# Last layer of a four-layer convolution and attention kernel: bias rows in the third group, six fillings before the third convolution, two convolutions in the third gathering step

## The chip, the core and the metric

The kernel runs as one program on one core of a Trainium2 chip. The metric is the device time of one execution in microseconds (us). The times shown are of three runs and of one profiled execution.

The engines are named as in the profile: PE is TensorE (PEld its weight loads), DVE is VectorE, ACT is ScalarE, POOL is GpSimd, SP is SyncE, which here only issues transfers.

## The reference

The input is one image of 512 channels and 64 x 64 pixels in float32. Four layers follow each other, each as `x = x + layer(group_norm(x))`: an attention by distances with 8 heads, two layers of gated depthwise 7 x 7 convolutions, and a linear attention. The change is in the last one:

```
qkv0 = affine(conv1x1(x, w_qkv))                 # 768 channels
agg  = affine(depthwise5x5(qkv0)) * w_pw*s_pw + b_pw
q, k, v = split(concat(qkv0, agg), 3)            # 512 channels each
q, k = relu(q) + eps, relu(k) + eps
z    = einsum(mean(k), q) + eps
vk   = einsum('bcn,bdn->bcd', v/sqrt(N), k/sqrt(N))
y    = einsum(vk, q) / z * g_norm + bt_norm + v
out  = affine(conv1x1(y, w_proj))
```

## The kernel before, in words

The image X (4 chunks of 128 channels, 4096 pixels) stays in SBUF. The last layer, `_linear_attention` (L1597), goes in these stages; a matmul in float32 stands in the trace as two records.

**Groups.** The 1 x 1 convolution to 768 channels is done for pairs of output chunks i = 0, 2, 4 and pairs of pixel blocks k = 0 to 3. One such pair of pairs is a "group (i,k)" of seven steps (`_Seven.steps`, in the order p1, p5, p2, p7, p6, p3, p4), each with two chunks of matmuls. Their operands are sums of weights (`w_sum`, made in `summed`) and differences of pixel blocks (`diff`, made in `differences`). The banks are `ps_vk` vk0 to vk3, one to each of the four sums of a group, and the next group takes them again. The results are kept (`keep`, L1789, ACT, in the pool tmp of 7 buffers), combined (L518, L522) and put (L1162 on ACT; L1169 and L1172 on DVE) into planes, which are stored to DRAM tensors G (L1151) by ACT or POOL.

**The list of steps.** From group (0,1) on the 77 steps lie in one list, `made`, in the order (0,1), (0,2), (0,3), (2,3), (2,2), (2,1), (2,0), (4,0) to (4,3). A group can bring a list of other pieces, one to a step (`also`); a piece is run just ahead of its step. `fill(n)` runs the next n steps of the list.

**Convolutions.** The depthwise 5 x 5 convolution of chunk i, half image hf, is `conv(i, hf)`: twelve of them, each in two parts of 128 matmul records. Each part takes two loads (`_PlaneConv.load`): taps T, a gathered S from G (L1198, issued by SP), and two shifted copies of S inside SBUF, one on ACT (L1205) and one on DVE (L1203). After a part its two banks (`ps_mm`, 4 in all) are transposed to the tile `turned` (L1259), and after the second part in four pieces on to the tiles `agg` (L1268); ACT then scales these (L1874). `convs(units, between)` runs convolutions, and after each part the next piece of `between`. The agg, w_sum, diff, k and q tiles come from one pool, kv, of 33 buffers.

The order is: 29 fillings; convolutions (0,0) and (1,0) with five fillings after each of their four parts; four fillings; convolutions (2,0) and (3,0) with six after each part; then (0,1), (4,0), (5,0) with 16 "early" products of v and w_proj between their parts, 1, 3, 3, 3, 3, 3. Then come the gathering steps q = 0 to 3 of the first half, each of four steps (`step`): a transposition of k and v blocks (L1930), the products vk of the step before, and a product with w_proj. Steps q = 0, 1, 2 hold one convolution each, (1,1), (2,1), (3,1), and q = 3 holds (4,1) and (5,1). The steps of the second half follow with no convolution, and then the output.

**Bias of the projection.** `pbias` is the sum over w_proj rows times bt_norm, scaled and shifted. `bias_row` and `row` load 128 x 512 rows through POOL's queue into the tmp pool; `bias(o)` multiplies (L1696) and reduces (L1697) one, `added` (L1699) finishes. `scaled_out` (L1680) multiplies w_proj by the row `s_row`, loaded by ACT's queue into a buffer of its own. The rows are loaded with group (2,2) and the biases made with (2,1), between the parts of the first two convolutions.

**Order of instructions.** Matmuls and a few others are pinned to the order in which the program names them (`keep_in_program_order`). All other instructions are put in order on their engines by the framework, which also places the tiles in the pools' buffers and adds the waits.

Of the kernel before, what the change touches and what calls it, by code (L numbers as in the profile page):

```python
# [10 lines left out]
FP = mybir.dt.float32  # L11
# [5 lines left out]
P = 128  # L17
# [1077 lines left out]
class _PlaneConv:  # L1095
# [117 lines left out]
    def conv(self, i, hf, wT, finish, dst, primed=False):  # L1213

        nc, f = self.nc, self.f
        if not primed:
            self.ahead(i, hf, wT)
        for r0 in range(0, f.nr, f.rounds):  # L1220
            ps = [self.psum.tile([P, BLK], FP, tag="mm", name="ps_cv") for _ in range(2)]
            for r in range(r0, r0 + f.rounds):
                if r % f.run == 0 and r > r0:
                    yield
                if r % self.nl == 0:
                    if r + f.rounds < f.nr:
                        self.ready.append(self.load(i, hf, wT, r + f.rounds))
                    w, S = self.ready.pop(0)
                for b in range(f.by * f.bx):
                    by, bx = divmod(b, f.bx)  # L1230
                    for rho in range(2):
                        rows = ts(rho, 64)
                        for g in range(4):
                            self.matmul(
                                ps[rho][ts(g, 32), ts(r - r0, f.n)].rearrange(
                                    "p (r w) -> p r w", w=f.w
                                ),
                                w[rows, r % self.nl, g, b, :],
                                S[rows, r % self.nl, g, :].rearrange(
                                    "p (r w) -> p r w", w=f.fw  # L1240
                                )[:, by : by + f.part, bx : bx + f.w],
                                start=(b == 0),
                                stop=(b == f.by * f.bx - 1),
                            )
            for rho in range(2):
                c0 = (rho * f.nr + r0) * f.ch
                if f.parts == 1:
                    out = dst.rearrange("p (l b c) -> p c b l", l=f.planes, c=32)[
                        :, c0 : c0 + f.rounds
                    ]  # L1250
                    src = ps[rho].rearrange("p (r b l) -> p r b l", r=f.rounds, l=f.planes)
                else:
                    out = self.turned[:, :, :, c0 : c0 + f.rounds * f.ch].rearrange(
                        "p b l (r c) -> p r b l c", c=f.ch
                    )
                    src = ps[rho].rearrange(
                        "p (r b l c) -> p r b l c", r=f.rounds, l=f.planes, c=f.ch
                    )
                nc.vector.transpose(out, src)  # L1259
            if r0 + f.rounds < f.nr:  # L1260
                yield
        for q in range(4):
            if f.parts == 1:
                d = dst[:, ts(q, N // 4)]
                nc.vector.transpose(d, d)  # L1265
            else:
                d = dst[q]
                nc.vector.transpose(  # L1268
                    d.rearrange("p (h x r w) -> p x r w h", h=2, x=f.phx, r=f.part),
                    self.turned[:, :, ts(q, f.phx), :].rearrange("p b l c -> p l b c"),  # L1270
                )
            finish(d)
            if f.parts == 1 or q == 3:
                yield
# [322 lines left out]
def _linear_attention(ctx, tc, a, X, vcol, vall, ident, gmask, small, centered, stats, norm, F, Z, out):  # L1597
# [45 lines left out]

    with ExitStack() as st:

        kvp = st.enter_context(tc.tile_pool(name="kv", bufs=33))
        ps_vk = st.enter_context(tc.tile_pool(name="ps_vk", bufs=1, space=PSUM))
        ps_mm = st.enter_context(tc.tile_pool(name="ps_mm", bufs=4, space=PSUM))
        pc = _PlaneConv(st, tc, f, F, ps_mm, NL, 4, True, nc.gpsimd, 2)
# [14 lines left out]
        def weights(i):  # L1664
# [6 lines left out]
        pbias = small.tile([P, NC], FP, tag="pbias", name="pbias")  # L1671
        step_p = small.tile([P, NC // 2], FP, tag="step_p", name="step_p")

        s_row = lq.tile([P, C], FP, tag="s_row", name="s_row")
        nc.scalar.dma_start(
            out=s_row, in_=bass.AP(a["L3_sp"].tensor, a["L3_sp"].offset, [[0, P], [1, C]])
        )

        def scaled_out(c):
            nc.vector.tensor_mul(w_proj[:, c], w_proj[:, c], s_row)  # L1680

        w_bt = []

# [75 lines left out]
        def summed(i):  # L1759
            ss = [kvp.tile([P, BLK], FP, tag="kv", name="w_sum") for _ in range(2)]  # L1760
            ss = [
                t.rearrange("p (n c m) -> p n c m", n=2, c=2)[:, n] for t in ss for n in range(2)
            ]
            wsum[i] = ss
            for _ in seven.sums(nc.vector, w_qkv[i], w_qkv[i + 1], ss):
                pass

        def differences(k, eng):

            def begin():  # L1770
                t = [
                    [flat(kvp.tile([P, BLK], FP, tag="kv", name="diff")) for _ in range(2)]
                    for _ in range(4)
                ]
                diff[k] = t, seven.differences(eng, view(k), t)

            def piece(n):
                if n == 0:
                    begin()
                for _ in range(2):  # L1780
                    next(diff[k][1])

            return [lambda n=n: piece(n) for n in range(4)]
# [11 lines left out]
        def group(i, k, also=()):  # L1795

            steps = []

            def begin():
                steps.extend(  # L1800
                    seven.steps(
                        w_qkv[i], w_qkv[i + 1], wsum[i], diff[k][0], view(k), bank,
                        lambda j, ps: keep(i, j, ps),
                        lambda m, n, ps, more: put(i + m, 2 * k + n, ps, more),
                    )
                )

            def step(n):
                if n == 0:
                    begin()  # L1810
                if n < len(also):
                    also[n]()
                steps[n]()

            return [lambda n=n: step(n) for n in range(7)]

        def centers(k):
            return [lambda: taken(2 * k), lambda: taken(2 * k + 1)]
# [24 lines left out]
            [lambda: taken(2), lambda: taken(3), lambda: summed(0)] + differences(1, dve),  # L1843
        )
        centered.began()
        made = group(0, 1, centers(2) + differences(2, dve))
        made += group(0, 2, centers(3) + differences(3, dve))
        made += group(0, 3, [lambda: summed(2)])
        scales = [lambda c=c: scaled_out(c) for c in range(NC)]
        rows = [bias_row] + [lambda o=o: row(a["L3_w_projT"][:, o]) for o in range(2)]  # L1850
        biases = [lambda n=n: n % 2 or bias(n // 2) for n in range(2 * NC - 1)]
        made += group(2, 3, [more_weights] + scales)
        made += group(2, 2, differences(0, dve) + rows)
        made += group(2, 1, biases)
        made += group(2, 0, [lambda: summed(4)] + differences(2, pool) + [added])
        made += group(4, 0)
        made += group(4, 1, differences(3, pool))
        made += group(4, 2)
# [7 lines left out]
            return [lambda n=n: fill(n) for n in ns]  # L1866

        def conv(i, hf, primed):
            agg[i, hf] = [kvp.tile([P, BLK], FP, tag="kv", name=f"agg{i}") for _ in range(4)]

            def affine(t):
                late.append(
                    lambda: tc.keep_in_program_order(
                        nc.scalar.activation(  # L1874
                            t, t, AF.Relu if i < 2 else AF.Identity,
                            bias=beta[:, i : i + 1], scale=alpha[:, i : i + 1],
                        )
                    )
                )

            return pc.conv(i, hf, a["L3_T"], affine, agg[i, hf], primed)

        late = []

# [99 lines left out]
            early = [lambda o=o: part(o, 0, 2) for o in range(NC)]  # L1984
            return prepare, turned, [lambda t=t: step(t) for t in range(QT)], early

        def both(*pieces):
            return lambda: [f() for f in pieces]

        def project_two(q0):  # L1990

            def v(c, n):
# [75 lines left out]

        fill(29)
        convs([(0, 0), (1, 0)], fills(5, 5, 5, 5))  # L2070
        fill(4)
        blks = {(hf, q): gather(hf, q) for hf in range(2) for q in range(4)}

        def prepare(hf, q):
# [5 lines left out]
        def steps(hf, q):  # L2080
            return list(blks[hf, q][2])

        convs([(2, 0), (3, 0)], fills(6, 6, 6, 6))

        early = [f for q in range(4) for f in blks[0, q][3]]
        convs(
            [(0, 1), (4, 0), (5, 0)],
            [
                early[0],
                both(*early[1:4]),  # L2090
                both(*early[4:7], prepare(0, 0)),
                both(*early[7:10]),
                both(*early[10:13]),
                both(*early[13:]),
            ],
        )
        vkp = [ps_vk.tile([P, C], FP, tag=f"vk{c}", name=f"vkp{c}") for c in range(NC)]
        for q in range(3):
            s = steps(0, q)
            convs([(q + 1, 1)], [s[0], both(prepare(0, q + 1), s[1])] + s[2:], 1)  # L2100
        s = steps(0, 3)
        convs(
            [(4, 1), (5, 1)],
            [s[0], s[1], both(prepare(1, 0), s[2]), turned(1, 0, 0, 1), s[3]],
            1,
        )

        km = wp.tile([P, NC], FP, tag="km", name="km")
        kmb = wp.tile([P, NC, 32], FP, tag="kmb", name="kmb")
# [327 lines left out]
```

## Time and profile before

| | us |
|---|---|
| three runs | 3759.53, 3754.57, 3759.23 |
| median | 3759.23 |
| profiled execution | 3754.97 |
| its span | 3753.1 |
| TensorE busy | 3689.7 (98%) |
| VectorE busy | 2751.0 (73%) |
| ScalarE busy | 2058.1 (55%) |
| POOL busy | 181.7 (5%) |

The mean granted TensorE clock is 0.996. The last layer by stages, in us of the span:

| stage | from | to | PE busy | DVE busy | granted clock | GB/s |
|---|---|---|---|---|---|---|
| groups (0,1) to (2,3) | 3176.2 | 3224.3 | 48.10 | 33.78 | 1.00 | 139 |
| convolutions (0,0), (1,0) | 3224.3 | 3270.3 | 40.06 | 30.79 | 0.93 | 166 |
| four fillings, convolutions (2,0), (3,0) | 3270.3 | 3340.7 | 68.09 | 45.51 | 0.98 | 176 |
| (0,1), (4,0), (5,0) | 3340.7 | 3382.8 | 39.82 | 29.81 | 1.00 | 188 |
| gathering, first half | 3382.8 | 3509.5 | 121.79 | 82.83 | 0.99 | 104 |
| gathering, second half | 3509.5 | 3628.0 | 118.50 | 57.59 | 1.00 | 44 |
| output | 3628.0 | 3753.1 | 119.14 | 98.52 | 1.00 | 111 |

How to read it: a line of the timeline gives the start, the length, the engine, the line of the code, the operation, the output and its inputs, the number of records, and in brackets the idle time ahead of it with what ended it. A busy time below the length of a stage is idle time of that engine. The granted clock is a share of TensorE's full clock.

### The profile page before, as it was taken

The page shows a single profiled execution, that of the slowest core. Times are in us where ns is not written, and L with a number is a line of the kernel's source. Part 1 is how long each engine was busy: PE and PEld are TensorE (multiplying, and loading weights), DVE is VectorE, ACT ScalarE, POOL GpSimd, SP SyncE. Part 2 cuts the span into 40 slices and gives each one's busy share as a digit, 9 for nine tenths or more (in the row PEclk, how much of TensorE's full clock was granted, in tenths as well). Part 3 has the DMA queues.
Part 4 walks back from the last instruction along what each step waited for, and adds up shares of the span by engine and source line. Part 5 has one row for each costly group of instructions (what it writes and reads, how often), then busy time and mean ns, then how long its engine had stood idle before and what let it go on. Part 6 is the DMA issues. An engine that isn't in the chain of part 4 may idle for free. (4 is left out here: it accounts for less than half of the span.)

```text
span 3753.1 us, 81702 instructions
## 1 busy us (share of the span) xinstructions
PE 3689.7 (98%) x35096; PEld 1713.3 (46%) x35096; DVE 2751.0 (73%) x3593; ACT 2058.1 (55%) x2994; POOL 181.7 (5%) x174
## 2 busy tenths in 40 slices
PE   7999999999999999999999999999999999999999
PEld 6544444444464444444333344554445544455543
DVE  6677777777766777777778767776777678666648
ACT  3577774777735777747557546662356632354210
POOL 1000000000000000010000000000000000232222
PEclk9999999999999999999999999999999999999999
DMA  2000000000000000000000026762057620564322
GB/s 102 10 7 7 4 7 12 7 4 7 7 4 10 7 7 4 7 12 7 4 4 7 4 73 196 199 191 60 22 180 196 190 87 31 157 184 111 88 65 93
DMA packets 183470, 222.73 MB, mean 59 GB/s; under 512 B 15800, under 2 KB 124600, under 8 KB 182976
## 3 DMA queue, kind: packets, MB, share of 16 engines
q1 hardware_dynamic: 158752, 158.36, 15.3%
q10 hardware_dynamic: 21312, 48.03, 3.5%
q0 software_dynamic: 3040, 11.08, 0.8%
q8 instruction: 277, 4.54, 0.5%
q14 instruction: 89, 0.73, 0.1%
HBM read 157.51 MB, written 59.90 MB: 58 GB/s over the span
## 5 line engine op out<-in xcount | busy, mean ns | idle before, releaser
L844 ACT ACTIVATE pt<-ps_s,A 128x512 f32<-128x512 f32 x2048 | 1286.2, 687 | 446.9 <-PE ps_s L836 436.8
L836 PE MATMUL ps_s<-O,K 64*64 64x512 f32 x8192 | 1419.3, 589 | 0.0
L1017 DVE TENSOR_TENSOR acc<-acc,pt 128x1024 f32<-128x1024 f32 x960 | 1178.0, 1227 | 324.8 <-ACT pt L844 299.0
L856 PE MATMUL av<-pt,O 64*64 64x512 f32 x4096 | 747.2, 589 | 0.0
L856 PE MATMUL av<-pt,V 64*64 64x512 f32 x4096 | 673.6, 589 | 0.0
L836 PEld LDWEIGHTS ps_s<-O,K 64*64 64x64 f32 x8192 | 438.4, 133 | 514.3 <-issue 464.2
L1205 ACT COPY S<-S 32x1295 f32<-32x1295 f32 (+1 forms) x272 | 341.8, 1256 | 223.0 <-DMA S<-F 107.8
L856 PEld LDWEIGHTS av<-pt,O 64*64 64x64 f32 x4096 | 238.4, 133 | 250.0 <-issue 237.2
L856 PEld LDWEIGHTS av<-pt,V 64*64 64x64 f32 x4096 | 209.3, 133 | 268.4 <-issue 254.0
L1128 PE MATMUL ps<-diff,w_sum 128*128 128x512 f32 x516 | 245.5, 608 | 8.8 <-DVE plane L1172 5.5
L1128 PEld LDWEIGHTS ps_cv<-S,T 64*32 64x32 f32 x13824 | 195.1, 106 | 113.4 <-issue 70.4
L1128 PE MATMUL ps_cv<-S,T 64*32 64x128 f32 x13824 | 234.2, 274 | 7.5 <-issue 2.5
L1128 PE MATMUL ps<-h,w_out_L 128*128 128x512 f32 x512 | 229.6, 600 | 1.5 <-DVE X L1488 1.4
L472 DVE TENSOR_TENSOR diff<-X 128x512 f32<-128x512 f32 x200 | 133.3, 682 | 69.0 <-PE ps L1128 36.8
L400 ACT ACTIVATE X<-X,gn_less 128x512 f32<-128x512 f32 x118 | 75.2, 709 | 153.7 <-DVE gn_less L130 152.8
L1128 PE MATMUL ps<-X,w_in_L 128*128 128x512 f32 x304 | 145.9, 611 | 8.6 <-ACT kept L1410 5.7
L1128 PEld LDWEIGHTS ps<-diff,w_sum 128*128 128x128 f32 x516 | 95.4, 191 | 123.9 <-issue 110.5
L1128 PEld LDWEIGHTS ps<-h,w_out_L 128*128 128x128 f32 x512 | 94.0, 190 | 118.3 <-issue 96.5
L1259 DVE STREAM_TRANSPOSE h<-ps_cv 128x512 f32<-128x512 f32 x112 | 109.3, 1049 | 49.8 <-PE ps_cv L1128 49.3
L1128 PE MATMUL ps<-h,pw_L 128*128 128x512 f32 x320 | 143.7, 599 | 1.7 <-DVE h L1476 1.4
L472 DVE TENSOR_TENSOR diff<-X,diff 128x512 f32<-128x512 f32 x200 | 134.7, 683 | 10.5 <-PE ps L1128 10.4
L1128 PE MATMUL vkp<-kT,vT 128*128 128x512 f32 x256 | 115.2, 592 | 0.0
(284 smaller groups left out, 3361.5 us busy)
## 6 DMA issues: line engine op xcount, KB each, us to landing
T<-in_L_T_dram SPq DMA_DIRECT2D x112, 384.0 KB, 4.2
F<-plane ACTq DMA_DIRECT2D x112, 324.0 KB, 3.5
S<-F SPq DMA_DIRECT2D x224, 162.0 KB, 4.6
S<-G SPq DMA_DIRECT2D x96, 153.0 KB, 4.6
row<-G SPq DMA_DIRECT2D x48, 272.0 KB, 3.3
T<-in_L_T_dram SPq DMA_DIRECT2D x48, 256.0 KB, 4.0
G<-plane POOLq DMA_DIRECT2D x33, 289.0 KB, 2.7
rd<-R SPq DMA_DIRECT2D x64, 128.0 KB, 2.9
```

What stands on the lines that cost most here:

```text
L400: return self.nc.scalar.activation(xs, xs, AF.Identity, bias=less)
L472: yield eng.tensor_tensor(t[j][c], a(c), b(c), ALU.subtract)
L836: nc.tensor.matmul(ps[ts(half, D), ts(h, BLK)], K[rows, t * P + half * D : t * P + (half + 1) * D], QO[pair][rows, cols], start=True, stop ...
L844: exp = nc.scalar.activation(pt[:, ts(h, BLK)], ps[:, ts(h, BLK)], AF.Exp, bias=A[:, t, h : h + 1])
L856: nc.tensor.matmul(av[half][rows, :], v[keys, t * P + h * D : t * P + (h + 1) * D], pt[keys, ts(h, BLK)], start=(t == 0), stop=(t == NT - 1),)
L1017: add = nc.vector.tensor_add(acc, acc if u > 1 else first, pt)
L1128: self.tc.keep_in_program_order(self.nc.tensor.matmul(*args, **kw))
L1205: nc.scalar.copy(second, first)
L1259: nc.vector.transpose(out, src)
```

## The change

- The three row loads are attached to the last step of group (0,2); the four biases and their finish go to steps 2, 3, 5 and 6 of group (0,3). Empty pieces stand between them.
- The row `s_row` has no buffer of its own any more; ACT's queue loads it into a tmp buffer with the first step of group (2,3), and w_proj is multiplied by it with that group's steps 2 to 5.
- Six fillings in place of four stand between the second convolution (1,0) and the third (2,0); after the parts of (2,0) and (3,0) stand 6, 6, 5, 5 in place of four times 6.
- The early products are 1, 2, 3, 3, 3, 4.
- The third gathering step holds convolutions (3,1) and (4,1), the fourth only (5,1).
- An agg tile is taken from its pool only when its piece is transposed, not all four when the convolution begins; the pool kv has 34 buffers.

```diff
-                d = dst[q]
+                d = dst(q)
...
-        kvp = st.enter_context(tc.tile_pool(name="kv", bufs=33))
+        kvp = st.enter_context(tc.tile_pool(name="kv", bufs=34))
...
-        s_row = lq.tile([P, C], FP, tag="s_row", name="s_row")
-        nc.scalar.dma_start(
-            out=s_row, in_=bass.AP(a["L3_sp"].tensor, a["L3_sp"].offset, [[0, P], [1, C]])
-        )
+        def scale_row():
+            t = tmp.tile([P, C], FP, tag="tmp", name="s_row")
+            nc.scalar.dma_start(
+                out=t, in_=bass.AP(a["L3_sp"].tensor, a["L3_sp"].offset, [[0, P], [1, C]])
+            )
+            w_bt.append(t)
...
-            nc.vector.tensor_mul(w_proj[:, c], w_proj[:, c], s_row)
+            nc.vector.tensor_mul(w_proj[:, c], w_proj[:, c], w_bt[-1])
...
-        made += group(0, 2, centers(3) + differences(3, dve))
-        made += group(0, 3, [lambda: summed(2)])
...
-        biases = [lambda n=n: n % 2 or bias(n // 2) for n in range(2 * NC - 1)]
-        made += group(2, 3, [more_weights] + scales)
-        made += group(2, 2, differences(0, dve) + rows)
-        made += group(2, 1, biases)
-        made += group(2, 0, [lambda: summed(4)] + differences(2, pool) + [added])
+        made += group(0, 2, centers(3) + differences(3, dve) + [both(*rows)])
+        biases = [lambda o=o: bias(o) for o in range(NC)]
+        wait = [lambda: None]
+        made += group(
+            0, 3, [lambda: summed(2)] + wait + biases[:2] + wait + [biases[2], both(biases[3], added)]
+        )
+        made += group(2, 3, [both(more_weights, scale_row)] + wait + scales)
+        made += group(2, 2, differences(0, dve))
+        made += group(2, 1)
+        made += group(2, 0, [lambda: summed(4)] + differences(2, pool))
...
-            agg[i, hf] = [kvp.tile([P, BLK], FP, tag="kv", name=f"agg{i}") for _ in range(4)]
+            agg[i, hf] = []
+
+            def rows(q):
+                agg[i, hf].append(kvp.tile([P, BLK], FP, tag="kv", name=f"agg{i}"))
+                return agg[i, hf][q]
...
-        fill(4)
+        fill(6)
...
-        convs([(2, 0), (3, 0)], fills(6, 6, 6, 6))
+        convs([(2, 0), (3, 0)], fills(6, 6, 5, 5))
...
-                both(*early[1:4]),
-                both(*early[4:7], prepare(0, 0)),
-                both(*early[7:10]),
-                both(*early[10:13]),
-                both(*early[13:]),
+                both(*early[1:3]),
+                both(*early[3:6], prepare(0, 0)),
+                both(*early[6:9]),
+                both(*early[9:12]),
+                both(*early[12:]),
...
-        for q in range(3):
+        for q in range(2):
             s = steps(0, q)
             convs([(q + 1, 1)], [s[0], both(prepare(0, q + 1), s[1])] + s[2:], 1)
+        s = steps(0, 2)
+        convs([(3, 1), (4, 1)], [s[0], s[1], both(prepare(0, 3), s[2]), s[3]], 1)
         s = steps(0, 3)
-        convs(
-            [(4, 1), (5, 1)],
-            [s[0], s[1], both(prepare(1, 0), s[2]), turned(1, 0, 0, 1), s[3]],
-            1,
-        )
+        convs([(5, 1)], [s[0], s[1], both(prepare(1, 0), s[2]), turned(1, 0, 0, 1), s[3]], 1)
```

More of the change, by code (lines that the diff above doesn't have):

```diff
@@ L1845, in _linear_attention, with both @@
         centered.began()
-        made = group(0, 1, centers(2) + differences(2, dve))
-        made += group(0, 2, centers(3) + differences(3, dve))
-        made += group(0, 3, [lambda: summed(2)])
+        def both(*pieces):
+            return lambda: [f() for f in pieces]
         scales = [lambda c=c: scaled_out(c) for c in range(NC)]
         rows = [bias_row] + [lambda o=o: row(a["L3_w_projT"][:, o]) for o in range(2)]
-        biases = [lambda n=n: n % 2 or bias(n // 2) for n in range(2 * NC - 1)]
-        made += group(2, 3, [more_weights] + scales)
-        made += group(2, 2, differences(0, dve) + rows)
-        made += group(2, 1, biases)
-        made += group(2, 0, [lambda: summed(4)] + differences(2, pool) + [added])
+        made = group(0, 1, centers(2) + differences(2, dve))
+        made += group(0, 2, centers(3) + differences(3, dve) + [both(*rows)])
[8 more added lines that the diff above has]
+        made += group(2, 0, [lambda: summed(4)] + differences(2, pool))
         made += group(4, 0)
@@ L1879, in affine @@
                 )
-            return pc.conv(i, hf, a["L3_T"], affine, agg[i, hf], primed)
+            return pc.conv(i, hf, a["L3_T"], affine, rows, primed)
         late = []
@@ L1985, in gather @@
             return prepare, turned, [lambda t=t: step(t) for t in range(QT)], early
-        def both(*pieces):
-            return lambda: [f() for f in pieces]
         def project_two(q0):
```

## The prediction, made before the changed kernel ran

> **What bounds the kernel now.** I read the page first: TensorE is busy for 98% of the span, so only its idle time and its slow stretches can be won. The change touches only the last layer (from 3161 us to the end), so next I asked whom TensorE waits for from 3060 us on:
>
> ```profile
> PE ps L1128 <- DVE plane L1172: 5.5, 1, 5.5
> PE ps_t L1930 <- ACT agg L1874: 2.7, 2, 1.5
> PE ps_cv L1128 <- DVE S L1203: 2.2, 2, 1.4
> PE ps_cv L1128 <- DVE turned L1259: 2.0, 2, 1.8
> ```
>
> (us in total, times, longest.) A handful of single waits, none of them a regular pattern. The timeline of TensorE places them; the brackets hold the idle time before a piece:
>
> ```profile
> 3243.05 1.98 PE L1128 MATMUL ps<-diff,w_sum 128*128 128x512 f32 x4 [0.43 <-DVE plane L1169]
> 3252.25 3.75 PE L1128 MATMUL ps<-diff,w_sum 128*128 128x512 f32 x4 [5.50 <-DVE plane L1172]
> ...
> 3284.93 0.42 PE L1128 MATMUL ps_cv<-S,T 64*32 64x128 f32 x8 [0.56 <-ACT S L1205]
> 3286.79 3.53 PE L1128 MATMUL ps_cv<-S,T 64*32 64x128 f32 x120 [1.43 <-DVE S L1203]
> ...
> 3385.17 0.33 PE L1930 MATMUL ps_t<-ident,agg 128*128 128x128 f32 x1 [1.46 <-ACT agg L1874]
> ...
> 3494.59 3.41 PE L1128 MATMUL ps_cv<-S,T 64*32 64x128 f32 x120 [0.17 <-DVE turned L1259]
> ...
> 3505.87 0.33 PE L1930 MATMUL ps_t<-ident,agg 128*128 128x128 f32 x1 [1.21 <-ACT agg L1874]
> ```
>
> (The piece before 3494.59, 8 records at 3493.99, waited 1.79 us for the same transposition.) After three of these stops the same work also runs longer: 3.75 us for four records that take 1.98, and 3.53 and 3.41 us for 120 records that take about 1.95 (128 take 2.04 to 2.08). The stages show why:
>
> ```profile
> 3252.25:3256.00 3.75, 3.75 (x12) 1.21 (x18) 3.72 (x4) 0.06 (x1) 3.44 (x4) 0.51 0.47 140
> 3286.80:3290.30 3.50, 3.50 (x121) 3.19 (x121) 0.80 (x2) 2.39 (x2) 0.00 (x0) 0.53 0.52 154
> 3494.60:3498.00 3.40, 3.40 (x121) 3.01 (x122) 0.31 (x1) 0.68 (x2) 2.01 (x3) 0.54 0.02 5
> ```
>
> (Third column from the right: granted clock.) It falls to about half for some 3.5 us, so each of these stops costs 1.5 to 1.8 us more than its idle time. [...]
>
> **Part 1: the bias rows leave the first two convolutions.** The order on VectorE ahead of the 5.50 us stop:
>
> ```profile
> 3239.09 0.78 DVE L1203 COPY S<-S 32x1207 f32<-32x1207 f32 x1 [4.75 <-DMA S<-G]
> 3239.90 0.69 DVE L1696 TENSOR_TENSOR bt<-bt 128x512 f32<-128x512 f32 x1
> ...
> 3251.31 0.80 DVE L1172 SCALAR_TENSOR_TENSOR plane<-ps,step_b,kept 128x256 f32<-128x256 f32 x2
> ```
>
> The bank that L1172 frees had been filled at about 3240.8, but VectorE works in order: it stood 4.75 us at a copy whose load had not landed and then ran without a pause. Two things in that backlog belong to the bias. Three multiplications and three reductions of rows lie between 3239.90 and 3246.37; by their distances to the next start (0.61, 0.59, 0.72, 0.61, 0.71, 0.61) they take 3.85 us. And the load landed late: the chain of waits gives S<-G 10.74 us, where the page has a median of 4.6. Four row loads of 256 KB went out at 3226.4 to 3228.6; 1.05 MB at the 172 GB/s of 3226 to 3260 is 6.1 us, just the difference. Without rows alone L1172 comes 3.85 us earlier and 1.65 us of the stop is left; with the earlier copy nothing is. What is late next is L1172 itself behind the four transpositions to agg, about 3243 to 3245, against a need at 3246.7. I take all: 0.43 + 5.50 + 1.77 = **7.7 us** (at least 0.43 + 3.85 = 4.3).
>
> Where the rows go: group (0,3), 3200.3 to 3212.3, and the scaling of w_proj to (2,3), up to 3224.3:
>
> ```profile
> 3200.30:3212.30 12.00, 12.00 (x30) 5.30 (x29) 5.60 (x12) 2.06 (x3) 1.14 (x3) 1.00 0.28 105
> 3212.30:3224.30 12.00, 12.00 (x29) 5.30 (x28) 7.08 (x14) 5.66 (x6) 1.98 (x4) 1.00 0.86 236
> ```
>
> (Columns: length, then PE, PEld, DVE, ACT, POOL busy, clock, DMA share, GB/s.) VectorE has 6.4 us free in the first and 4.9 in the second. Eight instructions at a spacing of 0.6 and four small ones at 0.2 make 5.6 us; four scalings at 0.6 make 2.4. Both fit. The scalings had cost nothing before, as they ran at 3081.7 to 3085.0, 130 us ahead of their place in the code. The instructions that are not pinned are ordered by the framework, so places in the code are not places in a queue.
>
> Waits that this adds, three. On VectorE a multiplication waits for its row; behind it stand the puts of (0,3), whose last bank TensorE wants at 3217.4, 4.2 us after L1172 does it now. On POOL the row loads wait for tmp buffers; behind them stand the plane stores, from which the first convolution loads at 3216.3. On ACT the scale row's issue (0.33 us) waits for a tmp buffer; behind it stands the copy "kept" of (2,3) at 3214.2 to 3214.9, which TensorE needs at 3215.7: 0.8 us of cover. The trace shows none of these waits; between 0 and about 6 us (stop and clock together), I take 0, since the buffers of the groups before are long free there.
>
> The scale row's 256 KB now fall into the stage with 0.86 DMA share: 1.1 us at its 236 GB/s. The last copy that the first part of the first convolution needs ends at 3224.3, for its second half at about 3227.1; it holds.
>
> **Part 2: six fillings.** A filling is 1.72 us of TensorE, so two more put 3.44 us between group (2,0) and the third convolution, which waits for loads of what (2,0) stored (S<-G issued at 3281.0, copies up to 3287). Waits of 0.56 + 1.43 us go, with 3.53 - 1.95 = 1.6 of clock: **3.6 us** (0 if the copy stays behind another instruction). The fillings in all stay the same (4 + 24 = 6 + 22).
>
> **Part 3: one product moved in the next step.** One product (1.72 us) goes from before (4,0) to behind (5,0). The wait of 1.46, and 0.28 after it, go. But (4,0) also waits for a store (issued 3338.8, its loads 3344.1): its waits of 1.01 and 0.77 us can grow by 1.72. I take the two as equal: **0** (from -1.7 to +1.7, with 1.6 more if the clock drops).
>
> **Part 4: two convolutions in the third gathering step.** Now the halves of (5,1) have only two turned blocks (0.87 us) between them, and the second waits 1.79 + 0.17 us for a transposition and loses 3.41 - 1.95 of clock. With a whole step between (6.0 us: 0.87 + 3.44 + 1.72) this goes: **3.4 us**. Behind (5,1) stand then two steps and the turned blocks, 12.9 us, in place of 6.0; the scaled agg came 7.8 us after the end of (5,1): the wait of **1.2 us** goes. The loads of (5,1) get the same cover as those of (2,1) and (3,1), which show no wait.
>
> The late allocation of agg and a 34th kv buffer only loosen: VectorE waits 1.26 us at 3404 for a free one, with no stop of TensorE behind it. I give it 0.
>
> **Sum.** 7.7 + 3.6 + 0 + 3.4 + 1.2 = 15.9 us. The profiled execution took 3754.97 us (span 3753.1 and 1.9 around it), so 3739.1 on its count. That execution is near the lowest of the three runs; the median, 3759.23, is 4.3 above it. The four known times average 3757.1, and from that I forecast **3741 us**.
>
> **Rivals.**
> 1. The moved rows put a stop into the third group. If the loads go out behind the last store of (0,2), at 3201.6, and need the longest landing seen, 10.0 us, the multiplications begin at 3211.6 and L1172 ends about 3218 to 3221 in place of 3213: 1 to 4 us too late, with 1.7 of clock. For it: the loads' median was 7.9 us. Against: half of VectorE is free. About 3746 us.
> 2. The change does not do what it says: the load behind the 4.75 us is late without the rows too, and the order that the framework makes keeps the copies ahead of the puts. Left are 4.3 us of part 1, 0 of part 2, 1.2 to 3.4 of the rest: 3750 to 3752.
> 3. Slower: agg's buffers are now taken when its transposition is written. If one is taken that TensorE still reads, VectorE stands in order, and the puts and bank releases behind it. A stop of that kind is priced by the one seen, 5.5 + 1.8 = 7.3 us; from 4 of the 12 convolutions on (29 us against 15.9) it is slower, about 3770. For it: two such waits of VectorE exist (1.26 and 0.25 us). Against: neither stops TensorE, and 34 buffers are one more.
>
> **How the numbers follow.** Forecast 0.55, rival 1 0.17, rival 2 0.13, rival 3 0.15. About 0.2%, 7.5 us, is what a measurement of this kernel can tell: the forecast and rival 1 are faster (0.72), rival 2 is no change (0.13), rival 3 slower (0.15). The range goes from 3735 (lowest run, part 3 a gain, small waits gone) to 3757 (the upper end of rival 2 with the spread of 5 us between runs), and leaves out rival 3.
>
> **What would show it.** Right: no wait of TensorE between (2,2) and (2,1), granted clock 1.00 from 3226 to 3500, S<-G of the second convolution landing in about 5 us, no wait before the third convolution or between the halves of (5,1), and L1696 at about 3203 to 3212. Wrong: a stop before (2,3)'s fourth step or the first convolution (rival 1), copies still standing at a late S<-G ahead of puts (2), idle time of VectorE ahead of L1268 with TensorE idle too (3).

## The result and the profile after

The kernel after takes 3750.2 us (median of 10 runs, 3745.49 to 3758.29) against 3757.24 us before (10 runs, 3752.64 to 3761.27). The ratio is 0.9982, with a 95% interval from 0.9973 to 0.999. So it is faster by some 7 us, where the prediction's sum was 15.9 us; the time is 9 us above the forecast of 3741 us and inside the range. The profiled execution took 3749.19 us (span 3747.5 us, granted clock 0.997).

First, whom TensorE waits for from 3060 us to the end, in the kernel after:

```profile
PE ps_cv L1128 <- DVE S L1203: 3.2, 2, 1.9
PE ps L1128 <- ACT kept L1791: 2.0, 1, 2.0
PE ps_cv L1128 <- DVE turned L1259: 2.0, 1, 2.0
PE ps L1128 <- DVE kept L518: 1.9, 1, 1.9
```

The 5.5 us behind L1172 are gone, and so are the 2.7 us behind agg but for 0.7. In their place stand four other waits of about 2 us. The timeline of TensorE gives their places:

```profile
3214.28 1.98 PE L1128 MATMUL ps<-diff,w_qkv 128*128 128x512 f32 x4 [1.95 <-DVE kept L518]
3250.18 2.83 PE L1128 MATMUL ps<-X,w_qkv 128*128 128x512 f32 x4 [2.03 <-ACT kept L1791]
3289.99 1.09 PE L1128 MATMUL ps_cv<-S,T 64*32 64x128 f32 x56 [1.30 <-DVE S L1203]
...
3348.34 1.76 PE L1128 MATMUL ps_cv<-S,T 64*32 64x128 f32 x72 [1.96 <-DVE turned L1259]
3352.03 1.93 PE L1128 MATMUL ps_cv<-S,T 64*32 64x128 f32 x56 [1.93 <-DVE S L1203]
3353.89 6.94 PE L1128 MATMUL ps<-agg,w_proj 128*128 128x512 f32 x12
```

In this order they are group (0,3), group (2,1), the third convolution (2,0), and the first part of (4,0), which stops twice: ahead of its first 72 records and ahead of its last 56. The 12 records at the end took 6.94 us, where the next 12 of the same kind (at 3362.77 us) took 5.42. In the kernel before, the same place had shorter waits:

```profile
3349.33 1.98 PE L1128 MATMUL ps<-agg,w_proj 128*128 128x512 f32 x4 [1.01 <-DVE turned L1259]
3353.33 1.09 PE L1128 MATMUL ps_cv<-S,T 64*32 64x128 f32 x56 [0.77 <-DVE S L1203]
3358.51 1.98 PE L1128 MATMUL ps<-agg,w_proj 128*128 128x512 f32 x4 [0.46 <-DVE turned L1259]
```

To see where the 7 us came from, I took the same landmarks in both timelines: the first matmul of the last layer, the first convolution, the first early product, the first transposition of gathering, the second half, and the output. Each stage in us:

| stage | before | after | difference | forecast |
|---|---|---|---|---|
| layer's start to the first convolution | 64.50 | 66.73 | +2.23 | 0 |
| to the first early product | 114.64 | 108.55 | -6.09 | -11.3 |
| to gathering | 42.04 | 46.54 | +4.50 | 0 |
| gathering, first half | 128.40 | 123.24 | -5.16 | -4.6 |
| gathering, second half | 114.08 | 114.08 | 0 | 0 |
| output | 127.83 | 125.17 | -2.66 | 0 |
| sum | 591.49 | 584.30 | -7.19 | -15.9 |

The sum of the profiled executions, 7.19 us, agrees with the medians. What lies ahead of the last layer isn't touched and starts it at 3158 to 3166 us from run to run; stages counted from the layer's own start leave that out. Each stage is still one execution of one kernel.

### The profile page after: what moved, and what is told of

Same layout as the page of the kernel before. It is cut to its first block, busy times and chain, and to the rows that moved or that the text cites. A ratio compares the mean times of both kernels' runs of the same rounds, so it can differ in the third digit from the quotient of the medians.

```text
span 3747.5 us, 81704 instructions
## 1 busy us (share of the span) xinstructions
PE 3689.1 (98%) x35096; PEld 1712.7 (46%) x35096; DVE 2746.8 (73%) x3593; ACT 2058.3 (55%) x2994; POOL 182.2 (5%) x174
```

## The experiments

Three places miss: a stop in (0,3) that is new, a stop in (2,1) in place of the old one, and the early products. The theory after this comparison was that the one moved early product is not free but is a good part of the miss, and that the stop in (2,1) has nothing to do with rows. The rivals were that (4,0) would stop in any case, and that the moved rows themselves hold things up.

### The early products as before

```diff
-                both(*early[1:3]),
-                both(*early[3:6], prepare(0, 0)),
...
+                both(*early[1:4]),
+                both(*early[4:7], prepare(0, 0)),
```

> The changed kernel with the early products between the convolutions (0,1), (4,0), (5,0) put back to 1, 3, 3, 3, 3, 3. Theory A (the product taken from before (4,0) is what the loads of (4,0) needed): the waits ahead of and inside (4,0), 1.96 + 1.93 us with some 3.1 us of half clock, shrink to about 1.0 + 0.8 without a loss of clock, the wait at the first gathering step grows from 0.7 to about 1.5; 4 us less than the changed kernel, about 11 us less than before. Theory B (the late agg tiles and the 34th buffer reorder the engines, and that is what costs): the waits at (4,0) stay above 3 us and the time is that of the changed kernel, 7 us less than before.

Measured: 3744.25 us (12 runs) against 3754.9 of the kernel before on the same chip, ratio 0.9971 (0.9963 to 0.998). That is a gain of 10.7 us where the kernel after has 7.0 against its own runs of before, so 3.6 us more. (The medians of before lie between 3753.76 and 3757.24 us on the chips used; I compare gains, each against its own, and not times.) The timeline of TensorE at the same place:

```profile
3342.28 1.98 PE L1128 MATMUL ps<-agg,w_proj 128*128 128x512 f32 x4 [1.71 <-DVE turned L1259]
3344.19 1.08 PE L1128 MATMUL ps_cv<-S,T 64*32 64x128 f32 x59
3346.02 1.09 PE L1128 MATMUL ps_cv<-S,T 64*32 64x128 f32 x56 [0.52 <-DVE S L1203]
```

The idle time is 2.65 us (1.71, 0.52 and 0.42 later on) in place of 3.89, and the clock stays up: the windows give a granted clock of 0.76 from 3347 to 3361 us in the kernel after,

```profile
3347.00:3361.00 14.00, 10.60 (x156) 5.67 (x164) 12.52 (x17) 9.11 (x13) 5.51 (x4) 0.76 0.82 183
```

and of 1.00 from 3334 to 3351 us here:

```profile
3334.00:3351.00 17.00, 14.52 (x279) 7.33 (x277) 10.41 (x15) 9.58 (x12) 5.62 (x4) 1.00 0.95 245
```

The stage to gathering takes 42.08 us, as before the change (42.04), and 41.7 to 43.4 us in the seven other kernels below that have the products at their old places. In the three that have the moved product it takes 46.54 (the kernel after), 46.15 and, with other fillings, 47.69 us. So part 3 costs 4.5 us in its stage: 1.2 us are longer waits (3.89 in place of 2.65), and most of the other 3.2 us are pieces that run longer at the lower clock: the 72, 56 and 12 records from 3348.34 to 3360.76 us take 10.49 us without the wait among them, where they take 7.95 here without theirs. (Three parts of 128 records outside that stretch take 2.33 to 2.38 us there and 2.03 to 2.08 here.) Behind the stage it gives 0.77 us back at the wait for agg (0.68 in place of 1.45). That leaves 3.7, near the 3.6 by the gains, though the intervals of the two gains (7.5 to 13.9 us and 3.8 to 10.1) overlap.

This profiled execution took 3740.02 us and is the second fastest of the twelve. It is also 3.5 us shorter than the kernel after ahead of the early products, where the two programs do not differ: the stops in (0,3) and (2,1) are 0.38 and 1.77 us there, and neither lost clock (1.98 us for the four records behind each).

### The bias at its old places

```diff
-        made += group(0, 2, centers(3) + differences(3, dve) + [both(*rows)])
...
+        made += group(2, 2, differences(0, dve) + rows)
+        made += group(2, 1, biases)
```

The rest is that of the kernel after, its early products too.

> The changed kernel with the bias rows, biases and their finish where they were before (groups (2,2), (2,1), (2,0)); the scale row and all else as changed. Theory A (moving the rows gains only about 2 us, because a wait of 1.95 us in group (0,3) and one of 2.0 us with 1.8 us of clock in group (2,1) take the place of 7.7 us): 2 us more than the changed kernel, the 5.5 us stop back, no stop in (0,3). My prediction's reading (7.7 us) would make it 8 us more, about the time of before.

Measured: 3749.1 us, ratio 0.9985 (0.9976 to 0.9993): a gain of 5.8 us against 7.0, no difference within the intervals. The largest stop of the kernel before is back, with its loss of clock (3.75 us for four records in place of 1.98), and the one in (0,3) is gone; the timeline of TensorE:

```profile
3249.68 3.75 PE L1128 MATMUL ps<-diff,w_sum 128*128 128x512 f32 x4 [5.50 <-DVE plane L1172]
```

Part 1 therefore takes a stop of 7.3 us (5.50 and 1.77 of clock) away and puts others in its place: in the kernel after 1.95 us in (0,3), and in (2,1) 2.03 us and 1.7 of clock. By the medians the move of the rows brings 1.2 us, which the intervals (3.8 to 10.1 us with it, 2.6 to 9.0 without) can't tell from nothing, nor from 5. The stages tell more. From the layer's start to the first early product the kernel after takes 175.28 us and this one 178.32. Of the profiles of this study with 29 fillings first and six before the third convolution, the four with the rows moved take 171.7 to 175.3 us there, the two with the rows at their old places 177.5 and 178.3. So the move saves some 2 to 7 us in these stages, and less than the 7.7 of the prediction in each pair.

### The kernel before without a bias

Of the kernel before, the row loads, the products and the sums of the bias are left out (the sums are set to zero, so the bias of the projection is missing in the output).

```diff
-        made += group(2, 2, differences(0, dve) + rows)
-        made += group(2, 1, biases)
+        made += group(2, 2, differences(0, dve))
+        made += group(2, 1)
```

> The kernel before, in which the bias of the projection is left out: no row loads, no multiplications and reductions, the sums set to zero (its output lacks that bias). It shows what moving the rows away can win at most. By the prediction the stop of 5.5 us in group (2,1) and its clock go wholly: 7.7 us less than before. Theory A (the plane stores, no longer late, now go out together with the loads of the second convolution, whose copies on ScalarE stand ahead of the copy that TensorE needs): a stop of about 2 us with up to 1.8 us of clock remains in (2,1), and 4 to 6 us are won.

Measured: 3749.37 us, ratio 0.9986 (0.9978 to 0.9995), a gain of 5.5 us. By the landmarks the stages up to the first early product take 174.06 us against 179.14, 5.1 us less. Even with no rows at all, a stop in (2,1) is there; TensorE's timeline of this kernel:

```profile
3247.98 2.84 PE L1128 MATMUL ps<-X,w_qkv 128*128 128x512 f32 x4 [2.72 <-ACT kept L1790]
```

So what takes the place of the 5.50 us stop belongs to the order of that group and not to the rows. It stands one step ahead of the old stop: the third step of (2,1) adds to the bank of the first, and waits until ScalarE has copied that bank to `kept`. ScalarE's timeline in the kernel after:

```profile
3248.22 1.20 ACT L1205 COPY S<-S 32x1207 f32<-32x1207 f32 x1 [7.57 <-PE ps L1128]
3249.45 0.69 ACT L1791 ACTIVATE kept<-ps,vec 128x512 f32<-128x512 f32 x1
```

A copy for the second convolution stands ahead of the `kept` that TensorE waits for. (The profile names a matmul as the end of that copy's wait here; in the kernel without a bias it names the load, S<-G, after a wait of 8.79 us.) POOL and SP show what stands around that copy's loads, in the timelines of the kernel after:

```profile
3240.99 0.54 POOL L1151 DMA_DIRECT2D G<-plane  x1 [10.51 <-DVE plane L1169]
3241.94 0.54 POOL L1151 DMA_DIRECT2D G<-plane  x1 [0.41 <-DVE plane L1169]
```

```profile
3242.44 0.85 SPq L1198 DMA_DIRECT2D S<-G  x2
```

Two plane stores go out 1.5 and 0.5 us ahead of the copy's loads. In the kernel before they went out 4 us behind these loads, since VectorE was late:

```profile
3242.80 1.74 POOL L1151 DMA_DIRECT2D G<-plane  x2 [14.19 <-DVE plane L1169]
```

```profile
3238.63 1.68 SPq L1198 DMA_DIRECT2D S<-G  x2
```

```profile
3242.53 1.20 ACT L1205 COPY S<-S 32x1207 f32<-32x1207 f32 x1 [0.38 <-DMA S<-G]
```

The copy there started 3.9 us after the issue, in the kernel after 5.8; the second load of the pair landed 4.1 us after its issue there, in the kernel after 6.0. A VectorE that is on time has moved the stores in front of the loads. Ten of the twelve profiles of this study divide in the same way: in the five with the second store issued 0.5 us ahead of the loads the copy started 5.5 to 6.5 us after the issue (5.53 with the early products as before, 5.78 in the kernel after, 6.47 without a bias), in the five with both stores some 4 us behind them 3.7 to 3.9 us after it.

### All rows at once, in kv buffers

The early products as before; all row loads go out together, into buffers of kv in place of tmp.

```diff
-            t = tmp.tile([P, C], FP, tag="tmp", name="bt")
+            t = kvp.tile([P, C], FP, tag="kv", name="bt")
...
-            if o + 2 < NC:
-                row(a["L3_w_projT"][:, o + 2])
```

> As the first (early products 1, 3, 3, 3, 3, 3), and all five bias rows loaded at once with group (0,2) into buffers of the kv pool, so that none waits behind plane stores on POOL. Theory A: VectorE's wait of 7.5 us for the third row goes and with it the 1.95 us stop of TensorE in group (0,3); 2 us less than the first kernel of this set. If the stop came from VectorE's load alone, it stays.

Measured: 3744.13 us (6 runs), ratio 0.9969 (0.9957 to 0.9981). The stop in (0,3) is gone in this execution, but 2.63 us stand at (2,1) and 2.79 + 0.74 us at (4,0): no gain over the 3744.25 us of the same chip with the rows in tmp. In the kernel after that stop comes from the third and fourth row: the program asks for them only with the first two biases (`bias` calls `row`), and their loads then stand on POOL behind the plane stores of (0,2):

```profile
3205.21 0.54 POOL L1151 DMA_DIRECT2D G<-plane  x1 [0.81 <-DVE plane L1172]
3205.78 1.13 POOL L1688 DMA_DIRECT2D bt<-in_L_w_projT_dram  x2
```

VectorE's timeline shows the multiplication waiting for them, with `kept` (L518), for which TensorE waits, behind it:

```profile
3212.33 0.69 DVE L1698 TENSOR_TENSOR bt<-bt 128x512 f32<-128x512 f32 x1 [7.53 <-DMA bt<-in_L_w_projT_dram]
3212.94 0.68 DVE L1682 TENSOR_TENSOR w_proj<-w_proj,s_row 128x512 f32<-128x512 f32 x1
3213.55 0.68 DVE L518 TENSOR_TENSOR kept<-kept,ps 128x512 f32<-128x512 f32 x1
```

The load took 6.5 us from its issue. The stop is not fixed: in the four other profiles with these loads at the same places the third row came 5.1 to 5.6 us after its issue, and the stop is 0.8 us or less (0.38 with the early products as before).

### Late agg buffers alone, then two convolutions in the third step on top

First, the kernel before with agg tiles taken late, the scale row in a tmp buffer and 34 kv buffers; second, that with (3,1) and (4,1) in the third gathering step and (5,1) in the fourth.

```diff
+        convs([(3, 1), (4, 1)], [s[0], s[1], both(prepare(0, 3), s[2]), s[3]], 1)
...
+        convs([(5, 1)], [s[0], s[1], both(prepare(1, 0), s[2]), turned(1, 0, 0, 1), s[3]], 1)
```

> The kernel before with only the buffers changed: agg tiles taken late, 34 kv buffers, the scale row in a tmp buffer with group (2,3). Steps, biases, fillings and gathering as before. Theory A: all stops of before stay (5.5 us in (2,1), 2.0 before the third convolution, 2.0 in (5,1), 1.2 behind it), and only the output stage gains what the changed kernel showed there (2.1 us of waits for VectorE): 2 to 3 us less than before. Prediction's reading: nothing, 0 us. Theory B (the buffers reorder the engines and cost): slower than before, new stops.

> As the first of this set, and the two convolutions in the third gathering step. Against that one the waits of 1.79, 0.17 and 1.21 us go, and a wait of 0.2 to 0.6 us comes: 2.6 to 3.0 us less by idle time. The prediction added 1.5 us of clock; theory A holds that a stop of 2 us costs clock only in some executions (it did not in the run without the bias), so the median gains 3 to 4 us.

Measured: 3753.41 us (11 runs), ratio 0.9991 (0.9982 to 1.0001), and 3748.24 us, ratio 0.9987 (0.9978 to 0.9997). By the medians the buffers bring about 1.5 us, which their interval can't tell from nothing; by the landmarks the output stage is 2.6 us shorter. That difference is steady: the stage takes 125.1 to 125.2 us in the nine kernels of this study with these buffers and 127.5 to 128.1 us in the three without. Two waits of the kernel before (from 3628 us) have no counterpart in any of the nine:

```profile
PE ps L1128 <- DVE y L518: 1.6, 1, 1.6
PE ps L1128 <- DVE y L2289: 0.5, 1, 0.5
```

The two convolutions bring 5.2 us by the medians of the same chip and 4.7 in their stage by the landmarks (128.5 us to 123.8, with a stop of 0.75 left): part 4 as forecast.

### The fillings alone, and all of them ahead of (0,1)

First, the kernel before with six fillings and 6, 6, 5, 5. Second, the kernel after with 6, 6, 10, 0, so that nothing stands between (3,0) and (0,1) and ten fillings between the two parts of (3,0).

```diff
-        convs([(2, 0), (3, 0)], fills(6, 6, 5, 5))
+        convs([(2, 0), (3, 0)], fills(6, 6, 10, 0))
```

> The kernel before with six fillings before the third convolution and 6, 6, 5, 5 after its parts; nothing else. Prediction: the waits of 2.0 us there and 1.6 us of clock go, 3.6 us less than before. Theory A (the copy on VectorE stays behind a result that is put first, as in the changed kernel): a wait of about 1.3 us stays, so 0.7 us less by idle time and at most 2.3 us.

> The changed kernel with 6, 6, 10, 0 in place of 6, 6, 5, 5, so that the second part of convolution (3,0), 2 us, stands behind the last group and before (0,1). Theory A: (4,0) gets 2 us more between the last stores and its first part, its waits shrink from 3.9 us with clock to about 1.9 without, and the short wait at the first gathering step stays at 0.7: 2 to 5 us less than the changed kernel, 3743 to 3746 beside 3750. If the waits at (4,0) are set by something else than this distance, nothing changes.

Measured: 3754.01 us, ratio 0.9997 (0.9988 to 1.0006): no difference that can be told. The third convolution still waits for the copy on VectorE, and (4,0) now stops with a loss of clock (3.68 us for four records that took 1.98 in the kernel before); TensorE's timeline of this kernel:

```profile
3291.75 1.09 PE L1128 MATMUL ps_cv<-S,T 64*32 64x128 f32 x56 [1.24 <-DVE S L1203]
...
3349.85 3.68 PE L1128 MATMUL ps<-agg,w_proj 128*128 128x512 f32 x4 [2.01 <-DVE turned L1259]
```

The two fillings that left the parts of (3,0) are missed at (4,0): the stage to gathering takes 43.10 us in place of 42.04. The second kernel took 3750.62 us, ratio 0.9988 (0.9979 to 0.9997), against an expectation of 3743 to 3746. (4,0) waits less (1.52 + 0.26 us), but (0,1) waits 1.62, 1.68 and 0.76 us: the wait has moved and the expectation failed.

### The first two convolutions one step later, and one earlier

Both have the early products as before. The first has 30 fillings ahead of (0,0), 7 ahead of (2,0); the second 28 and 9.

```diff
-        fill(29)
+        fill(30)
...
-        fill(6)
+        fill(7)
...
-        convs([(2, 0), (3, 0)], fills(6, 6, 5, 5))
+        convs([(2, 0), (3, 0)], fills(5, 5, 5, 5))
```

> The kernel after with the early products as before (1, 3, 3, 3, 3, 3) and the first two convolutions one step later: 30 fillings, 5, 5, 5, 5, then 7 fillings before the third convolution, then 5, 5, 5, 5 (77 in all, as before). Theory A: the stop of about 1.8 to 2.0 us in group (2,1) comes from the place of the convolution's loads and copies against the steps: ScalarE's copy S<-S of the second convolution, whose load shares the DMA engines with the plane stores of (2,2), stands ahead of the kept that TensorE waits for. With the convolution one step later both kept stand ahead of that copy on ScalarE, so this stop goes or is below 0.5 us, and with seven steps in place of six the wait of 1.3 us at the third convolution goes too: 3 us less than the same kernel with 29 and 6 fillings, about 3741 (ratio 0.9963). Theory B: the stop belongs to the loads themselves, whatever the order on ScalarE: late copies hold the second convolution itself or the next release, about 2 us stay as a wait of another instruction, and only the third convolution's 1.3 us may go: 3743 to 3745.

> The same, with the first two convolutions one step earlier: 28 fillings, 5, 5, 5, 5, then 9 before the third convolution, then 5, 5, 5, 5. Theory A: the plane stores of (2,2) come one step later against the second convolution's loads, which then have the DMA engines for themselves as in the kernel before, but the first convolution comes 1.7 us closer to the stores of (0,3) that it loads. The stop in (2,1) shrinks below 1 us, the third convolution's wait goes (nine steps); a new wait of up to 1.7 us at the first convolution: 3741 to 3744. Theory B: the stop stays at 1.8 to 2 us, 3743 to 3745.

Measured: 3739.27 us (5 runs), ratio 0.9964 (0.995 to 0.9977), and 3740.01 us (6 runs), ratio 0.9966 (0.9954 to 0.9978). These gains, 14.5 and 13.8 us, are the largest of the study and beat both kernels. In the first, what TensorE waits for from 3060 us on begins thus:

```profile
PE ps L1128 <- DVE turned L1259: 2.0, 1, 2.0
PE ps L1128 <- ACT kept L1791: 1.6, 1, 1.6
PE ps L1128 <- DVE kept L518: 0.7, 2, 0.4
```

The stop in (2,1) and the third convolution's wait are both gone, as theory A had it. (The 1.6 us are new, at 3303.70 us, between (2,0) and (3,0), and (4,0) loses 1.7 us of clock behind its stop of 1.98, with 3.18 us for four records in place of 1.98 and then 2.53 for 128 in place of 2.04; by the landmarks the last layer is 2.2 us shorter than with 29 and 6, where A had 3; by the gains it is 3.8.) But A's reason was right by half. ScalarE's timeline of this kernel:

```profile
3242.81 0.69 ACT L1791 ACTIVATE kept<-ps,vec 128x512 f32<-128x512 f32 x1 [4.46 <-PE ps L1128]
3244.35 1.20 ACT L1205 COPY S<-S 32x1207 f32<-32x1207 f32 x1 [0.85 <-DMA S<-G]
3245.57 0.69 ACT L1791 ACTIVATE kept<-ps,step_b 128x512 f32<-128x512 f32 x1
```

The `kept` that held TensorE (with `vec`) now stands ahead of the copy, but the other one still stands behind it. It does no harm there, as the copy starts 3.8 us after its loads' issue at 3240.55, not 5.5 to 6.5: here POOL's two stores went out from 3238.27 on, some 2 us ahead of the loads. In the second kernel the copy stands ahead of both; the timelines of ScalarE and SP:

```profile
3238.59 1.20 ACT L1205 COPY S<-S 32x1207 f32<-32x1207 f32 x1 [4.45 <-DMA S<-G]
3240.46 0.69 ACT L1791 ACTIVATE kept<-ps,vec 128x512 f32<-128x512 f32 x1 [0.67 <-PE ps L1128]
```

```profile
3234.72 2.01 SPq L1198 DMA_DIRECT2D S<-G  x2
```

POOL's two stores went out at 3234.94 and 3241.43, 0.2 and 6.7 us behind the issue of the first load; the copy started 3.9 us after the issue and was done before the bank was full. So the stop in (2,1) is gone here too, but for 0.66 us behind L1169, though the copy stands ahead of `kept` as in the kernel after. (The shift also puts the loads 1.7 us further ahead of that bank, so this run alone does not part the two reasons.) In this kernel 2.10 us stand between (2,0) and (3,0), (4,0) waits 2.25 + 0.50 us and agg 1.88, and by the landmarks its last layer is only 0.2 us shorter than with 29 and 6. Its profiled execution came to the last layer 3 us earlier, in code that is the same; how much of its gain is real is open.

## Why the prediction was wrong, point by point

- **Part 1 (7.7 us) is the step that failed.** The stop and its clock went as told, and for the reason told: the loads that VectorE had waited for landed 5.2 to 5.6 us after their issue in place of 9.7 to 10.7. But L1172, named as "late next", was not what came late; it was the `kept` of (2,1)'s first step, which the prediction had not looked for: with VectorE on time the plane stores get ahead of the second convolution's next loads, and a copy that comes 5.8 us after its issue holds `kept` on ScalarE. That gave 2.03 us back, and 1.7 us of clock (2.83 and 2.77 us for the next two pieces; 1.98 and 1.88 with the early products as before). With the kernel before freed of the bias the same stop is 2.72 us. By the landmarks, part 1 and part 2 together brought 6.1 us in their stage and not 11.3, and the rows took 2.2 of them back in the stage ahead. That the stop does not need the rows is shown by the kernel without any; that the stores ahead of the loads make the copy late is supported by the division of the profiles and by the versions with the convolutions one step later and earlier; holding back the stores alone wasn't tried.
- **The rows in (0,3), taken at 0, cost 2 us in the profiled execution** and 0.8 us or less in four others. It is rival 1's place, and its reason by half: two of the rows, not all, are issued behind the stores, because the program asks for them only with the first products. Its stop had no loss of clock (granted clock 1.00 from 3210 to 3217 us).
- **Part 2 (3.6 us) was too high.** The first copy is on time, the second on VectorE still comes 1.3 us late, as the prediction's bracket (0 if the copy stays behind another instruction) allowed. Alone it is worth about 1 us (3754.01 against 3754.96, no difference by the interval), and the two fillings are missing at (4,0).
- **Part 3 (0, from -1.7 to +1.7, with 1.6 more for the clock) cost 3.6 to 4.5 us.** The prediction let the wait for a bank and that for the store balance one another. But the waits around (4,0) grew from 2.65 us (with the new fillings and the old places of the products; 2.24 in the kernel before) to 3.89, and a drop of the clock came with them (0.76 from 3347 to 3361 us), which cost more than the growth of the waits, some 2.5 us (12 records took 6.94 us and not 5.42, and the pieces between ran longer too), while only 0.8 us came back at agg. The range of this step ended at 3.3; what it had too small is the price of the clock, 1.6.
- **Part 4 (3.4 + 1.2 us) was right**: 5.2 us by the landmarks of the first half, of which 0.8 is the shorter wait for agg that part 3 brought; 4.7 to 5.2 us where it is put on top of the late buffers.
- **The kv buffers (0) brought 2.7 us** in the output stage, where the prediction hadn't looked for a wait that they could loosen: VectorE's `y` came 1.6 and 0.5 us late there. How the buffers set this isn't shown; 34 buffers, the late taking and the scale row in a tmp buffer weren't separated. For the forecast this was luck: without it the time would have been further off.
- **The clock terms** (1.77, 1.6 and 1.46) were read as belonging to each stop. In the runs of this study stops of 1.7 to 2.8 us occur with the drop and without it: 1.79 + 0.17 us cost 1.46 in the kernel before, about 0.6 with the late buffers alone (2.55 us for 120 records in place of 1.97), and nothing with the fillings alone, where the stop is the same. At (4,0) four records took 1.98 us behind a stop of 2.79 us (the rows in kv) and 3.68 us behind one of 2.01 (the fillings alone). So in these runs the length of such a stop did not tell whether it lost clock; what does is not shown. The five stops of 5.5 us each lost 1.77 us in the piece behind them (3.75 us for four records in place of 1.98), and in four of the five kernels the next 128 records took 2.44 to 3.21 us in place of 2.04.
- **Rival 3 fell**: VectorE's late taking of agg stopped nothing. Rival 2's time (3750 to 3752) was the nearest to the result, but its mechanism fell. A copy does still stand ahead of the puts on VectorE, which waited 3.52 us for its load; but that load was not late without the rows (5.2 to 5.6 us), and the old stop went.

## What to carry to other kernels

When a stop goes away because an engine is no longer late, list every transfer that this engine triggers and shift them by the same time: one of them may now go out just ahead of a load, as the two plane stores did here 1.5 and 0.5 us ahead of a load whose copy started 5.8 us after its issue and not 3.9. An instruction moved between two waits of the same kernel is not free until the wait that it leaves has been seen with less cover; here 1.72 us of product moved cost 4.5 in its stage. And a version with the parts undone one at a time tells in a few runs which parts pay: here the gathering step paid 5 us, the buffers 1.5 to 2.7, the rows 2 to 7 in their stages (1.2 by medians with wide intervals), the fillings alone about 1, and the moved product cost 4.

## What the runs showed that had not been expected

The same stop of 1.79 + 0.17 us in (5,1) lost 1.46 us of clock in the kernel before, where the granted clock was 0.54 behind it, about 0.6 us with the late buffers alone and none with the fillings alone, with the code around the stop unchanged. Single stops of 1.7 to 2.3 us lost between 0 and 1.7 us of clock in these runs, so a sum that counts 1.5 us for every such stop is near the upper end. And loads issued 0.5 to 1.5 us behind two plane stores reached their copies after 5.5 to 6.5 us, against 3.7 to 3.9 us with the stores 2 us ahead of the loads or 4 us behind them.
